# Reordered copies and shifts, and a gate and ranks of another shape, in a four-layer graph and expert kernel

## The chip, the cores and the metric

The kernel runs on one core of a Trainium2 chip. The metric is the device time of one execution in microseconds (us). The kernel before was timed in three runs. One further execution was recorded by the hardware profiler, and all views of the profile are of that one. The engines are named TensorE (PE; its weight loads are PEld), VectorE (DVE), ScalarE (ACT), GpSimd (POOL) and SyncE (SP, which here only issues loads and stores).

## The reference

Four layers work on x, 625 nodes with 512 values each, and each is added to x after a layer norm of its input:

```
x = x + gnn0(layernorm(x))    # hyperbolic graph convolution, twice
x = x + moe(layernorm(x))     # 8 experts, top 2 of a softmax gate, capacity 93
x = x + gnn1(layernorm(x))    # graph convolution, twice, relu between
x = x + attn(layernorm(x))    # 8 x 16 = 128 heads over 100 pooled keys, then a two-layer map
```

In gnn0 each row is mapped (`h = mobius_matvec(W, x)`), a bias is added in the hyperbolic sense (a scaled row plus a scaled bias row, here called the shift), and the rows of 10000 edges and of the nodes' own loops are summed with weights `dis[row] * dis[col]`, where dis is the degree to the power -0.5.

In moe, `probs = softmax(xf @ gate_w.T + gate_b)`; each node goes to its two best experts, and each expert takes the 93 nodes of the largest weight, those with a lower index first where weights are equal:

```
wm = where(routed, w_te, -1.0)
sel_w, sel_idx = top_k(wm.T, cap)
h = gelu(einsum('ecd,edh->ech', xf[sel_idx], w1) + b1)
out = einsum('ech,ehd->ecd', h, w2) + b2     # times sel_w, added back at sel_idx
```

In attn, for each head: `att = softmax(q k)`, `z = att vc`; over all heads z is normed by its l2 norm, scaled by wz_g1, and `h1 = silu(zn @ wz_w1 + wz_b1)` (16384 by 1024) follows, then a norm and `wz_w2`.

## The kernel before

[...] Instructions are recorded in the order of the code, some parts at a higher priority, and each engine runs its own queue in the order in which a scheduler has then put it. `order(later, sooner)` fixes the order of two instructions. `busy(ps, n, behind)` issues n matmuls whose result is not used.

**Adjacency counts (gnn0).** `one_hots(j)` takes the j-th column of 125 edges and lets VectorE build two fp16 tiles: `sh` (line 390), which marks the source of each edge, in a ring of 8, and `dh` (line 391), which marks the target. TensorE multiplies them with 5 matmuls a column into the `eps` banks (line 78 for all of the front's matmuls). There are 80 columns. The last 8 of the last group are built in `finished`: their one-hots first, then, at high priority, their products tile by tile, the row of degrees (`total`, `dps`, `dboth`, `ddigit`, `degs`), `dis`, and the tiles `digit` and `AT` of the adjacency matrix. Beside this `conv_in` prepares the rows: ScalarE scales `raw` (line 580) and VectorE adds the bias row times a factor (line 581, the shift), for 5 tiles. After `finished`, the rows are scaled by dis (line 486), and `agps` (line 592) multiplies AT by them.

**Experts' front (moe).** `xf` is the normed x, `xfT` its transpose (banks `trps`, line 296). For the gate, `gT` (512 by 8) is held as the weights and xfT is moved past it: `lps` (line 720), 8 by 375 and 8 by 250; ScalarE copies these to `lT` (line 721), and 5 transposes (line 723) bring them back to nodes by experts. VectorE adds the bias (`pr`, line 724), makes the softmax and marks the two best (`wm`, nodes by experts: weight or -1). Between these, on TensorE, stands work for the attention layer that needs nothing of it: transposes of the key weights (`wkps`, line 762, copied by ScalarE, line 763), `bops` (line 768) and `bbps` (line 780), which gives `hb`.

`ranked(e)` transposes expert e's column of wm to a row (`rowps`, line 795; `row`, line 797). Then for each tile of nodes two VectorE instructions over all 625 entries of the row count the nodes of a larger weight (`gt`, line 802), and those of an equal weight with a lower index (`eq`, line 805). For the latter, `before` (line 701, GpSimd, then line 703, VectorE) is a mask of 125 by 3125 in bf16. Their sum `rank` gives the slot of the node, and `take` (line 809) is the one-hot of slots. For expert 0, `gathered` multiplies xf by take (`xgps`, line 835) behind `busy` of 16 matmuls, and one copy takes the result to `xgT`. For the other experts the ranks run one expert ahead. `first_map` is line 865 (`hps`), `second_map` line 876 (`ops`).

**Attention.** 128 heads go in NB = 32 blocks of HB = 4. Iteration i of the loop records, in this order: loads for block i+1 (SP), `hidden(i-2)`, the transposes of heads 0 and 1 of block i-1, `folded(i)` (`kbps`, line 1151: keys through the query weights), `turned(i+1)`, then the four heads of block i-1, `prepared(i-1)`, and `scores(i)`:

```
for h in range(HB):
    valued = value(i - 1, h)
    if h + 2 < HB:
        transposes(i - 1, h + 2)
```

`transposes` (TensorE `atps`, line 1191) turns a head's attention, and ScalarE copies it to `attT` (line 1194, two copies of 375 and 250 columns). `value` multiplies (`zps`, line 1200, 4 records a head), ScalarE squares the result into `zs` (line 1203, one buffer), VectorE scales it into `zT` (line 1204), and GpSimd adds the square to `zsq` (line 1207; VectorE in the last block, line 1209). `prepared` makes sums and differences on VectorE: four of zT, and four over 1099 elements (lines 1214, 1215, 1217 and 1216, in that order), three of them into `zq`. `scores` are 40 matmul records `scps` (line 1164) in three groups; for each, VectorE adds `cb` into `att` (line 1165) and takes the maximum `a_top` (line 1167), and ScalarE the exponentials (line 1172). `hidden` is the large product with wz_w1 in a Strassen-like form: 98 small products `h1ps` (line 1263) of a block's zT and zq with wz or `wq`, its splits, which GpSimd makes (line 1223); VectorE adds the products to `hacc` (line 1275). At the start of a block's products TensorE reads zT twice and then zq of line 1216.

Of the kernel before, what the change touches and what calls it, by code (L numbers as in the profile page):

```python
# [28 lines left out]
DC = D // 128  # L29
# [139 lines left out]
def layers_kernel(  # L169
# [135 lines left out]
    def tp(t):  # L305
        return slice(t * P, (t + 1) * P)
# [7 lines left out]
    with ExitStack() as es:  # L314
# [58 lines left out]
        degs = big.tile([P, NT], F32, name="degs")  # L373
        V.memset(degs, 1.0)

        ahead = []

        def counting(first, last):

# [2 lines left out]
        def one_hots(j):  # L382

            sh = senders[j % HOT]
            dh = hot.tile([P, HALF], F16, tag="dh", name="dh")
            V.tensor_scalar(sh[:, :N], nodes, src_f[:, j : j + 1], None, op0=OP.is_equal)  # L390
            built = V.tensor_scalar(dh, nodes[:, :HALF], dst_f[:, j : j + 1], weight[:, j : j + 1],
                                    op0=OP.is_equal, op1=OP.mult)
            if j == AHEAD - 1:
                ahead.append(built)
            return j, sh, dh

        def counted(group, hots, i):
# [62 lines left out]
        def finished(group, columns):  # L460


            hots = [one_hots(j) for j in columns]
            both = work.tile([P, NT, HALF], I32, tag="both", name="both", bufs=1)
            with tc.high_priority():
                for i in (NT - 1, *range(NT - 1)):
                    for hot_pair in hots:
                        counted(group, hot_pair, i)
                    if i == NT - 1:
                        total = row_of(group)  # L470
                    A.activation(both[:, i, :], group[2][i][:P, :HALF], AF.Copy)
                    if i == 0:
                        degrees(total)

                        RP[0, NT].act(dis, degs, AF.Sqrt)
                        R.inverse(dis, dis)
                        for t in range(NT):
                            scaled(t, sent, dis)
            for i in range(NT):
                tiles_added(group[0], both, i, i + 1)  # L480
# [30 lines left out]
        def conv_in(k, turned, scale, inside, pieces, own=None, beside=None):  # L511
# [13 lines left out]
            for a, b in pieces:  # L525
# [52 lines left out]
                for t in range(a, b):  # L578
                    i = slice(t - a, t - a + 1)
                    A.activation(raw[:, t, :], raw[:, t, :], AF.Copy, scale=k1[:, i])  # L580
                    V.scalar_tensor_tensor(raw[:, t, :], b_row[k], x2[:, i], raw[:, t, :], op0=OP.mult, op1=OP.add)
            return raw, mapped

        def conv_out(raw, mapped, last):
# [89 lines left out]
    with ExitStack() as es:  # L674
# [19 lines left out]
        for piece in PIECES:  # L694
            for c in range(DC):
                transposed(psum, xfT[:, c, :], xf, c, pieces=(piece,), wait=None if c else (0, product))


        before = big.tile([P, NT, N], BF16, name="before")

        nc.gpsimd.iota(before, pattern=[[-P, NT], [1, N]], base=0, channel_multiplier=-1,
                       allow_small_or_imprecise_dtypes=True)
        V.tensor_scalar(before, before, 0.0, None, op0=OP.is_lt)
        slots = big.tile([P, CAP], F32, name="slots")
        nc.gpsimd.iota(slots, pattern=[[1, CAP]], base=0, channel_multiplier=0,
# [6 lines left out]


        pr = big.tile([P, NT, NE], F32, name="pr")
        lT = work.tile([NE, N], F32, name="lT", bufs=1)
        lps = psum.tile([128, 512], F32, tag="ps", name="ltps")
        for a, b in PIECES:
            ps = psum.tile([128, 512], F32, tag="ps", name="lps")
            for c in range(DC):
                T.matmul(ps[:NE, : (b - a) * P], gT[:, c, :], xfT[:, c, a * P : b * P], start=c == 0, stop=c == DC - 1)  # L720
            A.activation(lT[:, a * P : b * P], ps[:NE, : (b - a) * P], AF.Copy)
            for t in range(a, b):
                T.transpose(lps[:P, t * NE : (t + 1) * NE], lT[:, tp(t)], ident[:NE, :NE])
        V.tensor_tensor(pr, lps[:P, : NT * NE].rearrange("p (t e) -> p t e", e=NE),
                        gb[:, None, :].to_broadcast([P, NT, NE]), op=OP.add)
        top, tot = R.new("g_top"), R.new("g_tot")
# [48 lines left out]
            return product  # L775

        keys_map(range(1))
        ps = psum.tile([128, 512], F32, tag="ps", name="bbps")
        for g in range(G):
            T.matmul(ps[:L, :1], a1[:, g, :], bkT[:, g : g + 1], start=g == 0, stop=g == G - 1)  # L780
        V.tensor_tensor(hb, ps[:L, :1], a1b, op=OP.add)

        node = big.tile([P, NT], F32, name="node")
        nc.gpsimd.iota(node, pattern=[[P, NT]], base=0, channel_multiplier=1, allow_small_or_imprecise_dtypes=True)

# [2 lines left out]
        def ranked(e):  # L788


            row[e] = work.tile([P, N], F32, tag="row", name="row")
            for a, b in PIECES:
                ps = psum.tile([128, 512], F32, tag="ps", name="rowps")
                for t in range(a, b):
                    turned = T.transpose(ps[:P, (t - a) * P : (t - a + 1) * P],
                                         wm[:, t, e : e + 1].to_broadcast([P, P]), ident[:P, :P])
                A.activation(row[e][:, a * P : b * P], ps[:P, : (b - a) * P], AF.Copy)

            gt, eq = R.new("rk_gt"), R.new("rk_eq")
            for t in range(NT):  # L800
                junk = work.tile([P, N], F32, tag="junk", name="junk")
                V.tensor_scalar(junk, row[e], wm[:, t, e : e + 1], None, op0=OP.is_gt, op1=OP.add,
                                accum_out=gt[:, t : t + 1])
                junk = work.tile([P, N], F32, tag="junk", name="junk")
                V.scalar_tensor_tensor(junk, row[e], wm[:, t, e : e + 1], before[:, t, :], op0=OP.is_equal,
                                       op1=OP.mult, accum_out=eq[:, t : t + 1])
            R.add(rank[:, :, e], gt, eq)
            take[e] = work.tile([P, NT, CAP], F32, tag="take", name="take")
            V.tensor_tensor(take[e], slots[:, None, :].to_broadcast([P, NT, CAP]),
                            rank[:, :, e : e + 1].to_broadcast([P, NT, CAP]), op=OP.is_equal)  # L810
            return turned
# [13 lines left out]

        def gathered(e, behind=None):
            xgT[e] = work.tile([128, DC, CAP], F32, tag="xgT", name="xgT")
            ps = psum.tile([128, 512], F32, tag="ps", name="xgps")
            if e == 0:
                busy(ps, 16, behind)  # L830
            for c in range(DC):
                if e == 0:

                    for t in range(NT):
                        T.matmul(ps[:, c * CAP : (c + 1) * CAP], xf[:, t, c * 128 : (c + 1) * 128], take[e][:, t, :],
                                 start=t == 0, stop=t == NT - 1)
                    continue
                T.transpose(ps[:, c * CAP : (c + 1) * CAP], xg[e][:, c * 128 : (c + 1) * 128], ident[:CAP, :CAP])
            V.tensor_copy(xgT[e], ps[:, : DC * CAP].rearrange("p (c s) -> p c s", s=CAP))

# [67 lines left out]

        load(0)
        turned = ranked(0)  # L910
        gathered(0, keys_map(range(1, DC), turned))
        for e in range(NE):
            if e + 1 < NE:
                load(e + 1)
# [180 lines left out]
    with ExitStack() as es:  # L1095
# [89 lines left out]
        def transposes(b, h):  # L1185
            ps = banks("atps")
            if b == h == 0:
                busy(ps[:, 0], 13, folded.last)
            for k, (p0, p1) in enumerate(PIECES):
                for t in range(p0, p1):  # L1190
                    T.transpose(ps[:L, k, (t - p0) * P : (t - p0 + 1) * P], att[b][:, t, h * L : (h + 1) * L],  # L1191
                                ident[:P, :P])
            for k, (p0, p1) in enumerate(PIECES):
                A.activation(attT[h % 2][:, p0 * P : p1 * P], ps[:L, k, : (p1 - p0) * P], AF.Copy)  # L1194

        def value(b, h):
            g = b * HB // H
            ps = banks("zps")
            for u in range(2):
                T.matmul(ps[:, u, : 2 * QN], vc[:, g * DH : (g + 1) * DH], attT[h % 2][:, 2 * u * QN : 2 * (u + 1) * QN],  # L1200
                         start=True, stop=True)
            zs = work.tile([128, 2, 2 * QN], F32, tag="zs", name="zs", bufs=1)
            A.activation(zs, ps[:, :, : 2 * QN], AF.Square)  # L1203
            scaled = V.tensor_scalar(zT[:, h % 2 : 4 : 2, h // 2, :], ps[:, :, : 2 * QN], g1T[:, b * HB + h : b * HB + h + 1],  # L1204
                                     None, op0=OP.mult)
            if b < NB - 1:
                nc.gpsimd.tensor_tensor(zsq, zsq, zs.rearrange("p u s -> p (u s)"), op=OP.add)  # L1207
                return scaled
            return V.tensor_tensor(zsq, zsq, zs.rearrange("p u s -> p (u s)"), op=OP.add)
# [70 lines left out]
        for i in range(NB + 1):  # L1280
# [14 lines left out]
                turned(i + 1)  # L1295
            if i >= 1:
                for h in range(HB):
                    valued = value(i - 1, h)
                    if h + 2 < HB:
                        transposes(i - 1, h + 2)  # L1300
            if 1 <= i < NB:
                prepared(i - 1)
            if i < NB:
# [151 lines left out]
```

## Time and profile before

| | us |
|---|---|
| three runs | 2287.81, 2288.89, 2290.73 |
| median | 2288.89 |
| the profiled execution, its own time | 2287.9 |
| its span in the trace | 2286.1 |
| busy: PE, DVE, POOL, ACT | 2226.3, 1619.1, 992.1, 814.8 |

The span is the time from the first to the last recorded instruction; the execution's own time has 1.8 us more around it. A block of attention takes 50.32 us (the h1ps of one block starts at 1241.91 and of the next at 1292.23). The stretches that the change touches are, in the span of before, 66 to 110 us (one-hots and rows), 174 to 219 us (experts' front), 219 us to the end of the experts (later ranks), and 620 to 2187 us (the heads). In the rows, a name such as `zps<-attT,vc` is result and operands, xN the number of instructions, and `[.. <-..]` the idle time of the engine ahead of them with what ended it. In the groups of the page, `busy, mean ns | idle` follow the form. TensorE's granted clock is 1.00 of full speed in the experts' front and in the heads, 0.97 from 60 to 112 us.

### The profile page before, as it was taken

To read this page: it belongs to the slowest core of one execution; us is meant where nothing else is said; L and a number is where in the kernel's file an instruction comes from. 1 tells how busy PE (TensorE), PEld (TensorE's weight loads), DVE (VectorE), ACT (ScalarE), POOL (GpSimd) and SP (SyncE) were. 2 spreads that over 40 slices of the span, in tenths; PEclk is the share of its full clock that TensorE was granted. 3 is DMA by queue.
4 is the path that set the end of the run, shared out by engine and by line. 5 is a ranking of instruction groups with operands and counts; after the bars stand their busy time and mean duration, and the time that the engine had idled before them with its cause. 6 is when DMAs were issued, how large, how long until landed. Compare 5 with 4: busy or idle time off the path is not lost.

```text
span 2286.1 us, 34420 instructions
## 1 busy us (share of the span) xinstructions
PE 2226.3 (97%) x12812; PEld 1767.3 (77%) x12812; DVE 1619.1 (71%) x2303; ACT 814.8 (36%) x2773; POOL 992.1 (43%) x1063
## 2 busy tenths in 40 slices
PE   9999999999999999999999999999999999999987
PEld 6647666656788888888888888888888888888853
DVE  7846223233488888778888887788888778888782
ACT  3364111112334443343344334334433433344322
POOL 1000000200255666555566665555666565566531
PEclk9999999999999999999999999999999999999988
DMA  7002788670222222332222233222222332221110
GB/s 258 8 1 104 276 288 294 219 220 32 38 64 60 66 60 60 96 73 61 59 67 60 60 83 80 68 60 64 62 59 65 93 72 60 60 67 41 42 60 23
DMA packets 326026, 204.68 MB, mean 90 GB/s; under 512 B 275535, under 2 KB 279564, under 8 KB 321001
## 3 DMA queue, kind: packets, MB, share of 16 engines
q1 hardware_dynamic: 317371, 189.65, 28.3%
q10 hardware_dynamic: 3639, 7.56, 0.9%
q0 software_dynamic: 4848, 5.26, 0.8%
q8 instruction: 102, 1.67, 0.3%
q14 instruction: 66, 0.53, 0.1%
HBM read 197.18 MB, written 5.23 MB: 89 GB/s over the span
## 4 chain that ended last, share of the span: by engine, by line
PE 84%; DVE 6%; ACT 4%; POOL 2%; issue 2%; DMA 1%; POOLq 0%; ACTq 0%; SPq 0%; DVEq 0%
PE h1ps L1263 35%; PE scps L1164 18%; PE hps L865 5%; PE kbps L1151 5%; PE ops L876 5%; PE zps L1200 3%; POOL zsq L1207 2%; ACT zs L1203 2%; PE stps L959 2%; PE atps L1191 2%; PE l1ps L966 2%; PE agps L592 1%; DVE hacc L1311 1%; PE mxps L78 1%; PE eps L78 1%
## 5 line engine op out<-in xcount | busy, mean ns | idle before, releaser
L1275 DVE TENSOR_TENSOR hacc<-hacc,h1ps 128x942 f32<-128x942 f32 (+1 forms) x510 | 529.1, 1084 | 11.5 <-PE h1ps L1263 11.5
L1164 PE MATMUL scps<-keys,xnT 128*125 128x400 f32 x1280 | 435.1, 499 | 0.0
L1223 POOL TENSOR_TENSOR wq<-wz 128x256 f32<-128x256 f32 x248 | 241.3, 983 | 405.4 <-PE h1ps L1263 347.2
L1164 PEld LDWEIGHTS scps<-keys,xnT 128*125 128x125 f32 x1280 | 240.0, 188 | 185.0 <-issue 1.7
L1172 ACT ACTIVATE att<-att,a_top 125x100 f32<-125x100 f32 x640 | 231.9, 364 | 362.2 <-DVE a_top L1167 362.2
L1263 PE MATMUL h1ps<-zT,wq 128*128 128x157 f32 x1736 | 302.6, 296 | 0.0
L1263 PE MATMUL h1ps<-zq,wq 128*128 128x157 f32 x1736 | 302.5, 297 | 0.0
L1207 POOL TENSOR_TENSOR zsq<-zsq,zs 128x628 f32<-128x628 f32 x124 | 187.8, 1515 | 201.8 <-ACT zs L1203 201.8
L1263 PEld LDWEIGHTS h1ps<-zT,wq 128*128 128x128 f32 x1736 | 256.1, 189 | 0.0
L1263 PEld LDWEIGHTS h1ps<-zq,wq 128*128 128x128 f32 x1736 | 255.9, 190 | 0.0
L1194 ACT ACTIVATE attT<-atps 100x375 f32<-100x375 f32 (+1 forms) x256 | 92.7, 433 | 397.0 <-PE atps L1191 397.0
L1223 POOL TENSOR_TENSOR wq<-wz,wq 128x256 f32<-128x256 f32 x248 | 211.1, 851 | 19.4
L1204 DVE TENSOR_SCALAR zT<-zps,cols 128x628 f32<-128x628 f32 x128 | 111.6, 872 | 149.2 <-ACT zs L1203 147.8
L1183 ACT ACTIVATE att<-att,a_tot 125x100 f32<-125x100 f32 x620 | 170.2, 364 | 10.7 <-DVE a_tot L1173 10.7
L1200 PE MATMUL zps<-attT,vc 100*128 100x314 f32 x512 | 160.9, 436 | 10.7 <-ACT attT L1194 10.6
L1223 POOL TENSOR_TENSOR wq<-wsum,wq 128x256 f32<-128x256 f32 x186 | 161.6, 869 | 14.7 <-POOL wq L1223 0.3
L1223 POOL TENSOR_TENSOR wq<-wsum 128x256 f32<-128x256 f32 x186 | 136.1, 732 | 64.6 <-PE h1ps L1263 64.6
L1263 PE MATMUL h1ps<-zT,wz 128*128 128x157 f32 x992 | 152.5, 296 | 0.0
L1142 DVE STREAM_TRANSPOSE wqT<-wqraw 128x512 f32<-128x512 f32 x128 | 80.2, 681 | 101.0 <-PE kbps L1151 84.2
L1263 PEld LDWEIGHTS h1ps<-zT,wz 128*128 128x128 f32 x992 | 141.0, 189 | 9.1
L1203 ACT ACTIVATE zs<-zps 128x628 f32<-128x628 f32 x128 | 88.8, 694 | 125.0 <-POOL zsq L1207 111.2
L1200 PEld LDWEIGHTS zps<-attT,vc 100*128 100x128 f32 x512 | 87.4, 191 | 46.0 <-ACT attT L1194 27.0
(409 smaller groups left out, 3431.7 us busy)
## 6 DMA issues: line engine op xcount, KB each, us to landing
w<-in_L_ffn_w_dram SPq DMA_DIRECT2D x16, 4096.0 KB
wz<-in_L_ffn_wz_w_dram SPq DMA_DIRECT2D x32, 2048.0 KB
wqraw<-in_L_ffn_Wq_w_dram SPq DMA_DIRECT2D x512, 64.0 KB
cb<-qbias SPq DMA_DIRECT2D x32, 195.3 KB
wkv<-in_L_ffn_Wkv_w_dram SPq DMA_DIRECT2D x1, 4096.0 KB
W_raw<-in_L_gnn_W_dram SPq DMA_DIRECT2D x2, 1024.0 KB
w<-in_L_ffn_Wkv_w_dram SPq DMA_DIRECT2D x1, 2048.0 KB
l1w<-in_L_gnn_W_dram SPq DMA_DIRECT2D x2, 1024.0 KB
```

Source lines behind the costliest of these rows:

```text
L865: T.matmul(ps[:, i * CAP : (i + 1) * CAP], w1[e][:, c, hc * 128 : (hc + 1) * 128], xgT[e][:, c, :], start=c == 0, stop=c == DC - 1)
L876: T.matmul(ps[:CAP], hT[e][:, hc, :], w2[e][:, hc, :], start=hc == 0, stop=hc == HC - 1)
L1151: folded.last = T.matmul(ps[:, k, h * L : (h + 1) * L], wqT[b][h][:, (c + k) * 128 : (c + k + 1) * 128], kcT[:, b * HB // H, :], start=Tru ...
L1164: T.matmul(ps[:P, t - t0, : HB * L], xnT[:, c, tp(t)], keys[b][:, c, :], start=c == 0, stop=c == DC - 1)
L1172: A.activation(own, own, AF.Exp, bias=top[:, t, h : h + 1], accum_out=tot[:, t, h : h + 1])
L1183: A.activation(own, own, AF.Copy, scale=tot[:, t, h : h + 1])
L1200: T.matmul(ps[:, u, : 2 * QN], vc[:, g * DH : (g + 1) * DH], attT[h % 2][:, 2 * u * QN : 2 * (u + 1) * QN], start=True, stop=True)
L1203: A.activation(zs, ps[:, :, : 2 * QN], AF.Square)
L1207: nc.gpsimd.tensor_tensor(zsq, zsq, zs.rearrange("p u s -> p (u s)"), op=OP.add)
L1223: engine.tensor_tensor(to, x, y, op=OP.subtract)
L1263: T.matmul(ps[:, at % 6 // 3, at % 3 * QN : (at % 3 + 1) * QN], now[j][:, m * 128 : (m + 1) * 128], zquarter[b][j][:, place[i]], start=Tru ...
L1275: V.tensor_tensor(to, to, got, op=OP.add)
```

## The change

It has three parts.

1. In `value` for the second head, the transposes of the last head are recorded before the square, and the square is ordered behind the last head's copies.
2. The shifts of the rows (line 581 of before) are collected in a list, and each is ordered behind the last one-hot that was built.
3. In the experts' front: `before` is one mask of 125 by 125 in fp32. The gate holds the nodes (xfT) as weights and moves gT past them, 4 matmuls for each of 5 tiles, straight into nodes by experts; the copies to lT and the transposes are gone. A node's rank is counted in three parts: in the tiles in front of its own with "greater or equal", in its own tile and those behind with "greater", and in its own tile with "equal" times `before`. `bbps` is recorded behind `bops` and is what `busy` waits for, which has 3 matmuls for 16. The sum `hb` stands behind the last copy of xgT, and expert 0's xgT comes in four tiles with a copy each.

```diff
+            for op in shifted:
+                order(op, one_hots.last)
...
-        before = big.tile([P, NT, N], BF16, name="before")
+        before = big.tile([P, P], F32, name="before")
...
-        for a, b in PIECES:
-            ps = psum.tile([128, 512], F32, tag="ps", name="lps")
+        for t in range(NT):
             for c in range(DC):
-                T.matmul(ps[:NE, : (b - a) * P], gT[:, c, :], xfT[:, c, a * P : b * P], start=c == 0, stop=c == DC - 1)
-            A.activation(lT[:, a * P : b * P], ps[:NE, : (b - a) * P], AF.Copy)
-            for t in range(a, b):
-                T.transpose(lps[:P, t * NE : (t + 1) * NE], lT[:, tp(t)], ident[:NE, :NE])
+                T.matmul(lps[:P, t * NE : (t + 1) * NE], xfT[:, c, tp(t)], gT[:, c, :], start=c == 0, stop=c == DC - 1)
...
+            V.memset(ge[:, :1], 0.0)
             for t in range(NT):
+                own = wm[:, t, e : e + 1]
+                if t:
+                    junk = work.tile([P, N], F32, tag="junk", name="junk")
+                    V.tensor_scalar(junk[:, : t * P], row[e][:, : t * P], own, None, op0=OP.is_ge, op1=OP.add,
+                                    accum_out=ge[:, t : t + 1])
...
-                V.tensor_scalar(junk, row[e], wm[:, t, e : e + 1], None, op0=OP.is_gt, op1=OP.add,
+                V.tensor_scalar(junk[:, t * P :], row[e][:, t * P :], own, None, op0=OP.is_gt, op1=OP.add,
                                 accum_out=gt[:, t : t + 1])
...
-                V.scalar_tensor_tensor(junk, row[e], wm[:, t, e : e + 1], before[:, t, :], op0=OP.is_equal,
+                V.scalar_tensor_tensor(junk[:, tp(t)], row[e][:, tp(t)], own, before, op0=OP.is_equal,
                                        op1=OP.mult, accum_out=eq[:, t : t + 1])
+            R.add(gt, gt, ge)
             R.add(rank[:, :, e], gt, eq)
...
+            if e == 0:
+                for c in range(DC):
+                    ps = psum.tile([128, 512], F32, tag="ps", name="xgps")
+                    if c == 0:
+                        busy(ps, 3, behind)
+                    for t in range(NT):
+                        T.matmul(ps[:, :CAP], xf[:, t, c * 128 : (c + 1) * 128], take[e][:, t, :],
+                                 start=t == 0, stop=t == NT - 1)
+                    copied = V.tensor_copy(xgT[e][:, c, :], ps[:, :CAP])
+                return copied
...
+        turned = keys_map(range(1, DC), turned)
+        ps = psum.tile([128, 512], F32, tag="ps", name="bbps")
+        for g in range(G):
+            biased = T.matmul(ps[:L, :1], a1[:, g, :], bkT[:, g : g + 1], start=g == 0, stop=g == G - 1)
+            order(biased, turned)
+        last = gathered(0, biased)
+        order(V.tensor_tensor(hb, ps[:L, :1], a1b, op=OP.add), last)
...
+            turned_next = ahead() if ahead is not None else None
+            square = A.activation(zs, ps[:, :, : 2 * QN], AF.Square)
+            if turned_next is not None:
+                order(square, turned_next)
...
-                    valued = value(i - 1, h)
-                    if h + 2 < HB:
-                        transposes(i - 1, h + 2)
+                    valued = value(i - 1, h, (lambda: transposes(i - 1, 3)) if h == 1 else None)
+                    if h == 0:
+                        transposes(i - 1, 2)
```

More of the change, by code (lines that the diff above doesn't have):

```diff
@@ L374, in layers_kernel @@
         V.memset(degs, 1.0)
-        ahead = []
+        ahead, shifted = [], []
         def counting(first, last):
@@ L394, in one_hots @@
                 ahead.append(built)
+            one_hots.last = built
             return j, sh, dh
@@ L580, in conv_in @@
                     A.activation(raw[:, t, :], raw[:, t, :], AF.Copy, scale=k1[:, i])
-                    V.scalar_tensor_tensor(raw[:, t, :], b_row[k], x2[:, i], raw[:, t, :], op0=OP.mult, op1=OP.add)
+                    shifted.append(V.scalar_tensor_tensor(raw[:, t, :], b_row[k], x2[:, i], raw[:, t, :],
+                                                          op0=OP.mult, op1=OP.add))
             return raw, mapped
@@ L696, in layers_kernel @@
                 transposed(psum, xfT[:, c, :], xf, c, pieces=(piece,), wait=None if c else (0, product))
-        before = big.tile([P, NT, N], BF16, name="before")
-        nc.gpsimd.iota(before, pattern=[[-P, NT], [1, N]], base=0, channel_multiplier=-1,
-                       allow_small_or_imprecise_dtypes=True)
+        before = big.tile([P, P], F32, name="before")
+        nc.gpsimd.iota(before, pattern=[[1, P]], base=0, channel_multiplier=-1, allow_small_or_imprecise_dtypes=True)
         V.tensor_scalar(before, before, 0.0, None, op0=OP.is_lt)
@@ L714, in layers_kernel @@
         pr = big.tile([P, NT, NE], F32, name="pr")
-        lT = work.tile([NE, N], F32, name="lT", bufs=1)
         lps = psum.tile([128, 512], F32, tag="ps", name="ltps")
-        for a, b in PIECES:
-            ps = psum.tile([128, 512], F32, tag="ps", name="lps")
+        for t in range(NT):
             for c in range(DC):
-                T.matmul(ps[:NE, : (b - a) * P], gT[:, c, :], xfT[:, c, a * P : b * P], start=c == 0, stop=c == DC - 1)
-            A.activation(lT[:, a * P : b * P], ps[:NE, : (b - a) * P], AF.Copy)
-            for t in range(a, b):
-                T.transpose(lps[:P, t * NE : (t + 1) * NE], lT[:, tp(t)], ident[:NE, :NE])
+                T.matmul(lps[:P, t * NE : (t + 1) * NE], xfT[:, c, tp(t)], gT[:, c, :], start=c == 0, stop=c == DC - 1)
         V.tensor_tensor(pr, lps[:P, : NT * NE].rearrange("p (t e) -> p t e", e=NE),
@@ L777, in layers_kernel @@
         keys_map(range(1))
[L778 to L781, printed above, removed]
         node = big.tile([P, NT], F32, name="node")
@@ L797, in ranked @@
                 A.activation(row[e][:, a * P : b * P], ps[:P, : (b - a) * P], AF.Copy)
-            gt, eq = R.new("rk_gt"), R.new("rk_eq")
+            ge, gt, eq = R.new("rk_ge"), R.new("rk_gt"), R.new("rk_eq")
+            V.memset(ge[:, :1], 0.0)
             for t in range(NT):
+                own = wm[:, t, e : e + 1]
[3 more added lines that the diff above has]
+                                    accum_out=ge[:, t : t + 1])
                 junk = work.tile([P, N], F32, tag="junk", name="junk")
-                V.tensor_scalar(junk, row[e], wm[:, t, e : e + 1], None, op0=OP.is_gt, op1=OP.add,
+                V.tensor_scalar(junk[:, t * P :], row[e][:, t * P :], own, None, op0=OP.is_gt, op1=OP.add,
                                 accum_out=gt[:, t : t + 1])
                 junk = work.tile([P, N], F32, tag="junk", name="junk")
-                V.scalar_tensor_tensor(junk, row[e], wm[:, t, e : e + 1], before[:, t, :], op0=OP.is_equal,
+                V.scalar_tensor_tensor(junk[:, tp(t)], row[e][:, tp(t)], own, before, op0=OP.is_equal,
                                        op1=OP.mult, accum_out=eq[:, t : t + 1])
+            R.add(gt, gt, ge)
             R.add(rank[:, :, e], gt, eq)
@@ L827, in gathered @@
             xgT[e] = work.tile([128, DC, CAP], F32, tag="xgT", name="xgT")
+            if e == 0:
[8 more added lines that the diff above has]
+                return copied
             ps = psum.tile([128, 512], F32, tag="ps", name="xgps")
-            if e == 0:
-                busy(ps, 16, behind)
             for c in range(DC):
[L832 to L837, printed above, removed]
                 T.transpose(ps[:, c * CAP : (c + 1) * CAP], xg[e][:, c * 128 : (c + 1) * 128], ident[:CAP, :CAP])
@@ L910, in layers_kernel @@
         turned = ranked(0)
-        gathered(0, keys_map(range(1, DC), turned))
+        turned = keys_map(range(1, DC), turned)
[5 more added lines that the diff above has]
+        order(V.tensor_tensor(hb, ps[:L, :1], a1b, op=OP.add), last)
         for e in range(NE):
@@ L1193, in transposes, with value @@
             for k, (p0, p1) in enumerate(PIECES):
-                A.activation(attT[h % 2][:, p0 * P : p1 * P], ps[:L, k, : (p1 - p0) * P], AF.Copy)
-        def value(b, h):
+                copied = A.activation(attT[h % 2][:, p0 * P : p1 * P], ps[:L, k, : (p1 - p0) * P], AF.Copy)
+            return copied
+        def value(b, h, ahead=None):
             g = b * HB // H
@@ L1202, in value @@
             zs = work.tile([128, 2, 2 * QN], F32, tag="zs", name="zs", bufs=1)
-            A.activation(zs, ps[:, :, : 2 * QN], AF.Square)
+            turned_next = ahead() if ahead is not None else None
+            square = A.activation(zs, ps[:, :, : 2 * QN], AF.Square)
+            if turned_next is not None:
+                order(square, turned_next)
             scaled = V.tensor_scalar(zT[:, h % 2 : 4 : 2, h // 2, :], ps[:, :, : 2 * QN], g1T[:, b * HB + h : b * HB + h + 1],
```

## The prediction

> **What bounds the kernel now.** I read the busy shares first, then the chain that ended last, then three stretches of the chain beside the timeline: the attention loop, the experts' front and the build of the adjacency counts.
>
> ```profile
> PE 2226.3 (97%) x12812; PEld 1767.3 (77%) x12812; DVE 1619.1 (71%) x2303; ACT 814.8 (36%) x2773; POOL 992.1 (43%) x1063
> PE 84%; DVE 6%; ACT 4%; POOL 2%; issue 2%; DMA 1%; POOLq 0%; ACTq 0%; SPq 0%; DVEq 0%
> L1203 ACT ACTIVATE zs<-zps 128x628 f32<-128x628 f32 x128 | 88.8, 694 | 125.0 <-POOL zsq L1207 111.2
> L1200 PE MATMUL zps<-attT,vc 100*128 100x314 f32 x512 | 160.9, 436 | 10.7 <-ACT attT L1194 10.6
> ```
>
> TensorE works 97% of the span, so a change pays only where it closes a gap of TensorE's or shortens a chain that TensorE waits for. The last row is such a gap: zps waits for attT 10.6 us in all, 31 times, once a block. The row above it says why attT is late: ACT's square zs waits for GpSimd's sum of squares. One block in the chain of waits:
>
> ```profile
> 1224.48 1.53 POOL zsq L1207
> 1226.03 0.69 ACT zs L1203
> 1226.73 0.38 ACT attT L1194
> 1227.15 1.33 PE zps L1200 x4
> 1228.48 13.44 PE scps L1164 x40
> 1241.91 26.14 PE h1ps L1263 x196
> ```
>
> The second head's square starts at 1226.03, when zsq ends. The last head's copies, whose transposes ended at 1225.75, stand behind it on ACT's queue, and TensorE starts the last head's zps at 1227.15. The same block in the timeline, where h1ps begins:
>
> ```profile
> 1237.17 0.98 DVE L1165 TENSOR_TENSOR att<-scps,cb 125x800 f32<-125x800 f32 x1
> 1238.07 1.29 DVE L1215 TENSOR_TENSOR zq<-zq,zT 128x1099 f32<-128x1099 f32 x1
> 1239.28 1.30 DVE L1217 TENSOR_TENSOR zT<-zT 128x1099 f32<-128x1099 f32 x1
> 1240.49 1.29 DVE L1216 TENSOR_TENSOR zq<-zT,zq 128x1099 f32<-128x1099 f32 x1
> 1241.71 0.98 DVE L1167 TENSOR_REDUCE a_top<-att 125x8 f32<-125x800 f32 x1
> 1242.82 0.70 PE L1263 MATMUL h1ps<-zq,wz 128*128 128x157 f32 x4
> ```
>
> The zq of L1216 ends at 1241.79, and TensorE's third pair of products reads it at 1242.82: 1.03 us of slack. VectorE has run without an idle moment since 1231.39. A TensorE that comes earlier, or a VectorE that comes later, uses this slack up.
>
> **The attention loop, step by step.** The copies move ahead of the second head's square. They start when the transposes end: 1225.78 instead of 1226.62, two of 0.375 us, done at 1226.53. The first of the last head's zps, in a stream, follows the third head's at 4 x 0.267 = 1.07 us, at 1226.65, not 1227.15: 0.50 us, and the slow restart after the wait (1.33 us by the chain in place of about 1.23) gives 0.10 more. So TensorE reaches scps, and h1ps, 0.60 us earlier. Over 31 blocks this alone would be -18.6 us.
>
> Two things come later. First, the square waits behind the copies: 1226.41 instead of 1226.03 (between 0.35 and 0.50 later). zs has one buffer, and square, zsq, square, zsq run as one chain with GpSimd (the 1.53 and 0.69 above), so the last head's zs, and zT behind it, shift by the same 0.38. Second, the order of VectorE's instructions in the built program changes in all these blocks, which the diff doesn't say: a_top (L1167), in before behind that zq, now stands between the first zq and the second, and att ahead of the first. Ahead of the zq of L1216 there is thus one more instruction: spacing 0.90 us (att to zq, of 800 elements like a_top, is 1238.07 - 1237.17). It ends at 1241.79 + 0.38 + 0.90 = 1243.07, or 1242.94 with the spacings of each shape; I take 1242.94. TensorE arrives there at 1242.82 - 0.60 = 1242.22, and waits 0.72. With 0.05 for the release and 0.10 for the restart (as at zps) it goes on at 1243.10: **+0.28 us a block** against before. Range +0.15 (no restart cost) to +0.45 (0.13 later, square 0.04 later). The first such block had 0.55 of slack instead of 1.03: +0.75. Sum 30 x 0.28 + 0.75 = **+9.1 us**. Behind this point nothing else waits: att b, the next instruction of VectorE, shifts by about 0.35, and the third group of h1ps needs its bank 1.4 us after. GpSimd's splits and SP's loads keep their order and run ahead of need. In the last block the square of head 1 heads the chain into the final h1ps; the copy put in front of it costs 0.35 us: **+0.35**.
>
> **The experts' front.**
>
> ```profile
> 188.11 0.96 DVE L703 TENSOR_SCALAR before<-before 125x3125 bf16<-125x3125 bf16 x1
> 190.60 2.69 PE L720 MATMUL lps<-xfT,gT 128*8 128x375 f32 x8
> 197.06 0.20 DVE L724 TENSOR_TENSOR pr<-ltps,gb 125x40 f32<-125x40 f32 x1 [5.27 <-PE ltps L723]
> 201.83 1.49 PE L780 MATMUL bbps<-cols,a 128*100 128x1 f32 x16
> 203.19 0.79 PE L795 MATMUL rowps<-ident,wm 125*125 125x125 f32 x5
> 204.58 0.87 DVE L802 TENSOR_SCALAR_CACHE_REDUCE junk<-row,wm 125x625 f32<-125x625 f32 x1 [1.06 <-ACT row L797]
> 213.47 4.70 PE L835 MATMUL xgps<-take,xf 125*128 125x93 f32 x40 [0.57 <-DVE take L809]
> ```
>
> All of this lies on the chain. (1) The comparison at 188.11 shrinks from 3125 elements to 125 and moves ahead: the second half of the transposes comes 0.6 earlier (in the sum of the next step). GpSimd's iota that fills it shrinks too (2.81 us at 178.91), long before it is needed: nothing. (2) The gate: two groups of lps, two copies and five transposes become 20 matmuls with the nodes as weights (40 records, as 4 lps are 8). bbps is the nearest row: 16 records with 100 columns of weights and one moving column take 1.33 in the chain, 0.083 each; 0.104 for 125 columns, 4.2 us in all. [...] I follow the row. An ACT DMA issue (0.28) now stands ahead of the xfT copies, so the last xfT comes at about 191.5 (191.19). The gate ends at 195.1 and pr starts at 195.2: -1.85 (at 0.15 a record only -0.5). (3) The exponential stands behind one copy of w instead of two: -0.4. wm 202.3 becomes about 200.2. (4) bbps no longer stands ahead of rowps, which now waits for wm alone: 200.3, -2.9 in all. (5) Ranks: in before ten instructions at 0.787 spacing. 625/0.96 is 651 ns, so 0.136 is fixed. After: 14 instructions over 5 x 750 elements, 3.91 + 14 x 0.14 = 5.87, and one small sum 0.2. [...] -1.8. So xgps starts at 208.7: **-4.8**. TensorE's cover until then is bops 5.5, bbps 1.4 and the warm-up of 3 (0.7) behind rowps, ends at 208.7 too, so no gap opens that could lower the clock, but nothing more is to be gained there either. The hb sum behind them, the four small copies of xgT, the small memsets on VectorE and the b2 load issued earlier on ACT: 0 to -0.2. Weights' loads have slack behind bops, and the ranks of later experts lie beside hps (14.5 us an expert). Range -3.0 to -5.5.
>
> **The rows' shifts.**
>
> ```profile
> 77.27 3.40 DVE L581 SCALAR_TENSOR_TENSOR raw<-b_row,cv_x,raw 125x512 f32<-125x512 f32 x5
> 102.76 0.16 DVE L424 CAST dboth<-dps 125x3 int32<-125x3 f32 x1 [2.15 <-PE dps L78]
> ```
>
> They leave 77.27. VectorE builds a column in 0.58, TensorE uses it in 0.80, and the ring is eight deep, so VectorE was already waiting for slots there; only 1.15 of the 3.40 reach the last one-hot (99.49 becomes 98.34), and dboth. Behind it the five shifts fill the wait for the last counts, but two to three of them (0.66 each) stand between dboth, the degrees and the scaled rows, a chain that agps waits for at 109.39: +1.98 - 1.15 = +0.8; I take **+0.5**, range -1.2 to +1.2.
>
> **Sum.** 9.1 + 0.35 - 4.8 + 0.5 = +5.1. The profiled execution, 2287.9 (span 2286.1), becomes 2293.0; it lies 1.0 under the median 2288.9, so I predict **2294.0**.
>
> **Rivals.** A: the sum as above, chance 0.55; its own range is -1 to +9, 2288 to 2298. B, on the other side: VectorE's new order does not bind, because zq of L1216 is ready by 1242.22 (it decides at 0.72 us: if the chain from zs to zq is shorter by that). Then TensorE keeps its 0.60: -18.6 - 4.8 + 0.85, about 2266. For it: the row of 10.6 us and 31 waits; against: VectorE is gapless from 1231.39 on. Chance 0.15. C: the release costs nothing and the square is barely later, +0.15 a block: 4.6 + 0.35 - 4.8 + 0.5, 2290; or zq's end comes at the same time as TensorE, 2286. Chance 0.17. D: the wait is dearer (0.45 a block) or GpSimd and VectorE slow each other: +14 - 4 = +10, 2299. Chance 0.13.
>
> **Numbers.** 0.2% is 4.6 us, about what a measurement of this kernel can tell from no change. Slower by more: somewhat over half of A (0.35) and D (0.13), 0.48. Within: the rest of A (0.18) and most of C (0.13), 0.31. Faster: B, and the low part of C and A, 0.21. The range 2283 to 2302 leaves out B and the far ends.
>
> **To look for after.** Right: zps no longer waits for attT; h1ps waits for zq on VectorE about 0.7 a block; period 50.6 instead of 50.32; xgps at about 208.7 less what the shifts did. Wrong: no idle before h1ps' third pair and a period of 49.7; or shorter gaps of agps at 109.

## The result and the profile after

The changed kernel takes 2295.22 us (median of 8 runs, 2294.2 to 2297.73) against 2288.77 of before (8 runs): a ratio of 1.0032, 95% interval 1.0022 to 1.0041. That is 6.4 us slower. The prediction was 2294.0, slower. The profiled execution has a span of 2293.1 us.

The rows of the page that answer to those of before:

```profile
PE 2224.8 (97%) x12805; PEld 1773.0 (77%) x12805; DVE 1605.4 (70%) x2386; ACT 818.0 (36%) x2771; POOL 989.8 (43%) x1063
PE 67%; DVE 19%; ACT 6%; POOL 4%; issue 3%; DMA 1%; ACTq 0%; POOLq 0%; DVEq 0%; SPq 0%
L1216 ACT ACTIVATE zs<-zps 128x628 f32<-128x628 f32 x128 | 89.0, 695 | 114.7 <-POOL zsq L1222 100.7
L1212 PE MATMUL zps<-attT,vc 100*128 100x314 f32 x512 | 152.5, 430 | 0.1
```

The gap at zps is closed (10.7 us of idle time became 0.1), and still VectorE's share of the chain went from 6% to 19%. The chain of waits in a block shows how it runs now:

```profile
1224.66 0.76 ACT attT L1204 x2
1225.41 0.59 ACT zs L1216
1226.07 1.52 POOL zsq L1222
...
1237.30 0.90 DVE a_top L1177
...
1240.62 1.22 DVE zq L1231
1241.88 25.34 PE h1ps L1278 x188
```

The copies stand ahead of the square, a_top stands between the parts of zq, and h1ps goes on only when zq (line 1231, line 1216 of before) ends. The view of waits, with the sum, the number and the longest in us, has the price of that, 0.70 us in each of 31 blocks:

```profile
PE h1ps L1278 <- DVE zq L1231: 21.7, 31, 0.7
```

A block takes 50.67 us (50.32 before). In the experts' front, the timeline rows that answer to those of before:

```profile
194.52 0.20 DVE L722 TENSOR_TENSOR pr<-ltps,gb 125x40 f32<-125x40 f32 x1 [5.59 <-PE ltps L721]
201.10 0.73 PE L788 MATMUL rowps<-ident,wm 125*125 125x125 f32 x5
202.43 0.86 DVE L802 TENSOR_SCALAR_CACHE_REDUCE junk<-row,wm 125x625 f32<-125x625 f32 x1 [2.88 <-ACT row L790]
209.34 4.70 PE L836 MATMUL xgps<-take,xf 125*128 125x93 f32 x40
```

rowps has no idle time of TensorE's ahead of it: wm was ready at 199.56, and TensorE came at 201.10. The table by windows (us, busy time and instructions of PE, PEld, DVE, ACT, POOL, then the granted clock, the DMA share, GB/s) says why:

```profile
188.00:190.00 2.00, 1.89 (x18) 1.91 (x18) 0.94 (x3) 1.73 (x5) 0.00 (x0) 1.00 0.32 105
190.00:192.00 2.00, 2.00 (x18) 2.00 (x18) 0.00 (x0) 0.02 (x1) 0.00 (x0) 0.86 0.36 135
192.00:194.00 2.00, 2.00 (x11) 2.00 (x11) 0.00 (x0) 0.00 (x0) 0.00 (x0) 0.50 0.33 128
...
196.00:198.00 2.00, 2.00 (x11) 2.00 (x10) 1.90 (x5) 1.27 (x3) 0.00 (x0) 0.50 0.33 128
198.00:200.00 2.00, 2.00 (x19) 2.00 (x18) 1.42 (x7) 1.94 (x4) 0.00 (x0) 0.94 0.06 24
```

TensorE is busy in all but 0.11 us of these windows, but its clock falls to half while the gate's matmuls run, and 11 instructions fall into a window of 2 us instead of 18.

The two profiled executions also differ where the change touched nothing: before had TensorE at a clock of 0.57 from 33 to 36 us and 0.66 from 555 to 560 us, where the changed one had 1.00. That gave the changed execution 2.1 us by the end of the first group of counts (its `dboth`), and 1.8 more between the experts and the heads. It is a matter of the single execution, not of the change: e1, e2 and e3, whose code is before's in this stretch, reached the same mark 1.6 to 2.3 us earlier too. The experiments are therefore read stage by stage, each stage from a mark of its own.

### The profile page after: what moved, and what is told of

It reads as the page before. It is cut to its first block, busy times and chain, and to the rows that moved or that the text cites. A ratio compares the mean times of both kernels' runs of the same rounds, so it can differ in the third digit from the quotient of the medians.

```text
span 2293.1 us, 34516 instructions
## 1 busy us (share of the span) xinstructions
PE 2224.8 (97%) x12805; PEld 1773.0 (77%) x12805; DVE 1605.4 (70%) x2386; ACT 818.0 (36%) x2771; POOL 989.8 (43%) x1063
## 3 DMA queue, kind: packets, MB, share of 16 engines
q0 software_dynamic: 4848, 5.26, 0.8%
## 4 chain that ended last, share of the span: by engine, by line
PE 67%; DVE 19%; ACT 6%; POOL 4%; issue 3%; DMA 1%; ACTq 0%; POOLq 0%; DVEq 0%; SPq 0%
PE h1ps L1278 34%; PE hps L869 5%; PE kbps L1161 5%; PE ops L880 5%; POOL zsq L1222 4%; PE zps L1212 3%; PE atps L1201 3%; ACT zs L1216 3%; PE stps L969 2%; DVE zT L1229 2%; DVE zT L1232 2%; DVE zq L1231 2%; DVE zq L1229 2%; DVE zq L1230 2%; PE eps L78 2%
## 5 line engine op out<-in xcount | busy, mean ns | idle before, releaser
L1290 DVE TENSOR_TENSOR hacc<-hacc,h1ps 128x942 f32<-128x942 f32 (+1 forms) x510 | 534.5, 1085 | 36.0 <-PE h1ps L1278 31.8
L1193 ACT ACTIVATE att<-att,a_tot 125x100 f32<-125x100 f32 x620 | 170.1, 364 | 10.7 <-DVE a_tot L1183 10.7
L1212 PE MATMUL zps<-attT,vc 100*128 100x314 f32 x512 | 152.5, 430 | 0.1
L1161 PE MATMUL kbps<-kcT,wqT 128*128 128x100 f32 x1024 | 122.0, 277 | 0.3 <-DVE hacc L1290 0.3
```

The costliest lines, as they stand in the source:

```text
L1161: folded.last = T.matmul(ps[:, k, h * L : (h + 1) * L], wqT[b][h][:, (c + k) * 128 : (c + k + 1) * 128], kcT[:, b * HB // H, :], start=Tru ...
L1193: A.activation(own, own, AF.Copy, scale=tot[:, t, h : h + 1])
L1290: V.tensor_tensor(to, to, got, op=OP.add)
```

## The experiments

All were timed in five rounds beside before. Two stage times from the profile go with them: a block of the heads (zps to zps), and the front, from the end of the last agps to the first hps (40.03 us before, 37.57 in the changed kernel).

**e1, the copies alone**: the first part of the change, on the kernel before.

> The kernel before with the first part alone (last head's copies ahead of the second head's square). Theory (VectorE's new order binds: a_top ahead of the zq that TensorE reads third): TensorE waits about 0.70 us for that zq in each of 31 blocks, a block takes 50.67 us instead of 50.32, and the last block 0.35 more: +11.2, about 2300. Rival (the loop is neutral and the 6.4 us of the changed kernel come from elsewhere): 2289.

Measured: 2299.07, ratio 1.0049 (1.0035 to 1.0063), +10.7 us; 50.67 a block. The loss is that of the first part, and at the size of the theory. The cause was not yet shown by it.

**e2, the copies with zq first.**

```diff
+            zsums.third = V.tensor_tensor(to[2], z[0][1], to[1], op=OP.subtract)
...
+                peak = V.tensor_reduce(top[:, t0:t1, :].rearrange("p t h -> p (t h)"),
+                if b and t0 == 0:
+                    order(peak, zsums.third)
```

> As the copies alone, but the first a_top of each block is ordered behind that zq, as VectorE's queue had it before. Theory (order): zq is ready at about 1242.17 in the block of the prediction, TensorE comes at 1242.22: next to no wait, a block takes 49.7 to 49.8 us, -17 us, about 2272. Rival (the later square and the chain of squares behind it are what TensorE waits for, not the order): the wait stays at 0.4 or more and the time is 2284 or above.

Measured: 2300.6, ratio 1.0055 (1.0041 to 1.0068). My theory fell, by 28 us. The first block took 49.97 us, as the theory has it, but from the second on it was 50.71. The wait for zq was gone (0.20 was still lost there), and TensorE waited in another place, at the end of the block. Timeline rows of one block of e2, then the rows of before that answer to the first two, with its one wait for h1ps:

```profile
1229.14 0.87 DVE L1211 TENSOR_SCALAR zT<-zps,cols 128x628 f32<-128x628 f32 x1 [1.90 <-ACT zs L1208]
1252.47 0.28 DVE L1175 RECIPROCAL a_tot<-a_tot 125x20 f32<-125x20 f32 x1 [1.27 <-ACT att L1174]
1269.40 0.70 PE L1193 MATMUL atps<-ident,att 125*100 125x125 f32 x5
1270.30 0.74 PE L1193 MATMUL atps<-ident,att 125*100 125x125 f32 x5 [0.20 <-DVE hacc L1282]
1271.35 3.81 PE L1151 MATMUL kbps<-kcT,wqT 128*128 128x100 f32 x32 [0.30 <-DVE hacc L1282]
```

```profile
1226.76 0.87 DVE L1204 TENSOR_SCALAR zT<-zps,cols 128x628 f32<-128x628 f32 x1 [1.45 <-ACT zs L1203]
1250.10 0.28 DVE L1173 RECIPROCAL a_tot<-a_tot 125x20 f32<-125x20 f32 x1 [1.27 <-ACT att L1172]
1254.75 1.14 DVE L1275 TENSOR_TENSOR hacc<-hacc,h1ps 128x942 f32<-128x942 f32 x1 [0.26 <-PE h1ps L1263]
```

VectorE's second zT comes 0.45 later in the block than before (its idle time is 1.90, not 1.45), since the square does. From there to its last hacc its waits are for ScalarE and as long as in before (1.45 twice for zs, 1.27 for a_tot), so it is late at the end, and the transposes and kbps that reuse its banks wait. In before VectorE had only 0.26 us to spare in a block, the one time it waited for h1ps. In numbers: TensorE gains 0.60 at zps, loses 0.20 at zq, where it arrives at the very moment zq does, and 0.80 between atps and kbps (1.95 from start to start instead of 1.14): +0.40; the block grew by 0.39.

**e3, the order alone**: the second zq ordered behind the first a_top (`order(zsums.second, peak)`), nothing else.

> The kernel before with VectorE's order alone: a_top is ordered ahead of the second zq, the copies stay where they were. Theory (slack): zq comes 0.8 to 0.9 us later into 1.03 us of slack, TensorE does not wait, 50.32 us a block, 2289 (within 2). Rival (an instruction more ahead of zq costs its 0.9 us wherever it stands): +27, 2316.

Measured: 2294.55, ratio 1.0026 (1.0017 to 1.0035); a block 50.46, the first one 1.38 longer. Both expectations missed. zq ends 1.0 us later, and TensorE meets it: 0.03 of wait, and the second matmul behind it comes after 0.24 instead of 0.13 (the four take 0.80, in before 0.70):

```profile
1244.64 0.80 PE L1265 MATMUL h1ps<-zq,wz 128*128 128x157 f32 x4
```

These 0.14 in 30 blocks and the first block make the 5.6 us that the loop is longer. A slack that is used up to the last hundredth is not free.

**e4, the changed kernel with zq first**: the edit of e2 on the changed kernel.

> The changed kernel with the first a_top of each block ordered behind the zq. Theory (order): the changed kernel's 2295.2 less 31 times 0.9 us: about 2267, clear below before. Rival (the later square): 2284 or above.

Measured: 2293.34, ratio 1.0027 (1.0017 to 1.0037); 50.71 a block, as e2. So it is not VectorE's order that keeps the first part from paying; the order only decides where TensorE waits.

**e9, as e4, with a_tot later.**

```diff
+            shares[b] = V.reciprocal(tot, tot)
...
+                                if at == 6 * 5 and b + 1 in shares:
+                                    order(shares[b + 1], added_up)
```

> e4 (the changed kernel, zq ahead of the first a_top) with one thing more: a_tot, for which VectorE waits 1.27 us in e2 and e4 because ScalarE's exponentials aren't done, is ordered behind the fifth hacc of the block instead of the third. Theory (the block is a closed loop through VectorE, which is 0.45 late from the second square on and hands its banks back late): VectorE regains 1.27, TensorE is the bound again, 49.7 us a block, about 2263. Rival (VectorE's lateness isn't what holds e4): 50.7 us a block as in e4, 2293.

Measured: 2271.24, ratio 0.9924 (0.9911 to 0.9938); 49.90 a block. VectorE doesn't wait for a_tot any more, gives its banks back in time, and the 0.80 between atps and kbps are gone:

```profile
1242.37 0.27 DVE L1186 RECIPROCAL a_tot<-a_tot 125x20 f32<-125x20 f32 x1
1259.70 3.81 PE L1162 MATMUL kbps<-kcT,wqT 128*128 128x100 f32 x32
```

The block is -0.60 + 0.20 = -0.40 against before; the missing 0.20 to 49.7 is the meeting at zq, as in e2. The theory of the closed loop holds: VectorE's work of a block, once late at the squares, hands TensorE its banks back late.

**e8, two buffers for zs.**

```diff
-            zs = work.tile([128, 2, 2 * QN], F32, tag="zs", name="zs", bufs=1)
+            zs = work.tile([128, 2, 2 * QN], F32, tag="zs", name="zs", bufs=2)
```

> The kernel before with two buffers for zs instead of one; every engine's queue keeps its order (but for the last block). Theory (the block is a closed loop through VectorE, of which the chain of squares sets the start): squares no longer wait for GpSimd's sums, the second square runs at about 1225.1 of the block of the prediction instead of 1226.0 and the last scaled zT comes 1 to 3 us earlier, so neither attT nor VectorE holds TensorE: 49.7 us a block, -18 us, 2270. Rival (VectorE is bound by its own work, whatever comes first): 50.1 us or more a block, 2281 or above.

Measured: 2267.21, ratio 0.9912 (0.9898 to 0.9925), with no instruction moved in the blocks. The chain of a block:

```profile
1216.37 2.12 PE zps L1200 x8
1218.49 13.44 PE scps L1164 x40
1231.93 26.14 PE h1ps L1263 x196
1258.07 1.07 PE atps L1191 x10
1259.14 3.73 PE kbps L1151 x32
```

It is TensorE from end to end, 49.70 us. Squares follow zps at once, the copies follow in time, the last zT starts 2.7 us earlier in the block (6.33 instead of 9.03 after the first zps), and VectorE now waits for TensorE, not TensorE for it:

```profile
DVE hacc L1275 <- PE h1ps L1263: 59.3, 128, 0.5
```

**e10, the changed kernel with two buffers for zs.**

> The changed kernel with two buffers for zs (rk_ge takes the place of a tile no longer used, for room). Theory (one buffer, and the chain of squares that it makes, was what the moved copies delayed): 49.7 us a block with the copies ahead of the square too, e5 less 21, 2263. Rival (the copies ahead of the square cost by themselves, or VectorE's order does): 50.3 or more a block, 2284 or above.

Measured: 2262.71, ratio 0.9889 (0.9874 to 0.9904); 49.70 a block. With a second buffer the copies ahead of the square cost nothing, and gain nothing.

**e5, the second and third part without the first**: the changed kernel with the heads of before.

> The second and third part without the first: the changed kernel's front, the heads as before. Prediction's sum for these parts: 0.5 - 4.8 = -4.3, 2284.1. By the two profiles (the changed one has TensorE's clock at 0.50 from 191.4 to 198.6 us, and is only 2.4 us ahead behind the experts' front): +0.1 - 2.5 = -2.4, 2286.

Measured: 2284.07, ratio 0.998 (0.9971 to 0.9989), -4.6 us. In the profile the front is 2.47 us shorter (37.56). The rest of the 4.6 isn't in the stages that these parts touch; the interval reaches from -6.6 to -2.5.

**e6, the gate with more columns.**

```diff
+                T.matmul(lps[:P, t * 64 : (t + 1) * 64].rearrange("p (k e) -> p k e", e=NE), xfT[:, c, tp(t)],
+                         gT[:, c, None, :].to_broadcast([128, 64 // NE, NE]), start=c == 0, stop=c == DC - 1)
```

> As e5, but each matmul of the gate moves gT eight times over, 64 columns instead of 8, into 64 columns of the bank (the first 8 are used): the same number of matmuls and weight loads, with more of the array at work. Theory (the clock falls because TensorE's matmuls move 8 columns, so that it counts as idle): the clock stays at 1.0, a gate record takes 0.104 us, and expert 0 begins about 2.4 us earlier than in e5: 2283.6. Rival (the clock falls for another reason, such as the phase of the run or the weight loads): the clock falls to 0.5 here too and the time is e5's or, with wider matmuls, above it.

Measured: 2280.93, ratio 0.9966 (0.9954 to 0.9978). The front takes 34.87 us, 2.69 less than in e5. The windows over its gate and the wkps behind it:

```profile
191.00:193.00 2.00, 2.00 (x17) 1.90 (x18) 0.75 (x3) 0.96 (x3) 0.00 (x0) 1.00 0.32 108
193.00:195.00 2.00, 2.00 (x20) 2.00 (x20) 0.00 (x0) 0.00 (x0) 0.00 (x0) 1.00 0.36 135
195.00:197.00 2.00, 2.00 (x21) 2.00 (x21) 0.65 (x4) 0.80 (x3) 0.00 (x0) 1.00 0.33 128
197.00:199.00 2.00, 2.00 (x21) 2.00 (x20) 1.86 (x6) 2.00 (x5) 0.00 (x0) 1.00 0.33 128
```

The same number of matmuls with eight times the columns runs at full clock. That TensorE counts as idle under 8 columns was the theory's guess, and no run shows it. What the runs show is the clock: with the 8-column gate it is 0.50 in the windows from 192 to 198 us in the changed kernel, from 192 to 196 in e4 and e5 and from 194 to 200 in e9; with 64 columns it is 1.00 in all windows from 191 to 199 in e6 and from 188 to 200 in e11. With the old gate it is 1.00 from 186 to 214 in before and from 180 to 208 in e7; in e12 it is 0.50 from about 187.4 to 190.9, ahead of most of its gate, behind windows in which TensorE had worked only 1.64 of 3.40 us. So a half clock can fall into this stretch with the old gate too, but with the 8 columns it came in each of these four profiles, and with TensorE at work (2.00 of 2.00 us in every window at 0.50).

**e7, the old gate with the rest of parts 2 and 3.**

> As e5, but with the gate as before (gT as the weights, copies to lT, transposes). Theory (clock): no half speed in this stretch; the gate's own gain (-0.6 in the profile) is given up, and rowps, no longer held by TensorE at half speed, comes 1.5 to 2.5 earlier than in e5 for its queue and 0.6 later for wm: about e5 less 1, 2285. Rival (the new gate is worth its 1.85 us of the prediction): e5 plus 1.8, 2288.

Measured: 2283.27, ratio 0.9978 (0.9969 to 0.9987); front 36.64, 0.92 less than in e5, as the theory of the clock had it. The times of e5 and e7 do not tell the two apart. The gate's own worth shows against e6: 36.64 - 34.87 = 1.77 us.

**e12, the shifts alone**: the second part of the change, on the kernel before.

> The kernel before with the second part alone (shifts behind the one-hots). Prediction: +0.5 (-1.2 to +1.2). By the profiles of the changed kernel (0.15 later at agps than its lead at the first group of counts): +0.1, 2288.8. Rival (the shifts' 3.40 us come off in full): 2285.3.

Measured: 2287.26, ratio 0.9995 (0.9986 to 1.0004). From the first group of counts to the last one-hot it takes 43.65 us instead of 44.82, and to the ninth matmul record of agps 55.50 instead of 55.67. The 3.40 us do not come off; what does is mostly given back. How much isn't sure to some tenths: in the profiles of before, e1, e2 and e8, whose code is the same here, the second of these times runs from 55.65 to 56.31.

**e11, the parts that pay**: e6 with two buffers for zs, the heads otherwise as before.

> e6 (parts 2 and 3, wide gate) and e8 (two zs buffers) in one, heads otherwise as before. The two lie in different stretches, so their gains add: 2280.9 - 21.5 = 2259.5. Rival (TensorE, now without gaps in the heads, draws something else down): above 2263.

Measured: 2259.99, ratio 0.9874 (0.9859 to 0.9889): 28.5 us faster than before. The gains of e6 (7.8) and e8 (21.5) add up to 29.2, so they hardly touch each other. Its page:

```profile
PE 2213.9 (98%) x12805; PEld 1770.2 (78%) x12805; DVE 1633.4 (72%) x2386; ACT 813.7 (36%) x2771; POOL 991.9 (44%) x1063
PE 90%; DVE 5%; ACT 2%; issue 2%; DMA 1%; POOLq 0%; SPq 0%; DVEq 0%; ACTq 0%; POOL 0%
```

## Why the prediction was right, and where it was not

| term of the sum | predicted | measured |
|---|---|---|
| heads, 31 blocks | +9.1 | +11.6 (changed kernel), +10.7 (e1) |
| last block and behind | +0.35 | +0.33 to its third pair of h1ps, +1.8 to the last (changed kernel) |
| experts' front | -4.8 | -2.46, and -5.16 with the clock at 1.0 (e6) |
| shifts | +0.5 | +0.1 (changed kernel), -0.2 (e12) |
| sum | +5.1 | +6.4 |

**The heads: cause right, one term too small.** TensorE comes to scps 0.60 earlier (5.34 after the first zps instead of 5.95), as predicted. zq ends 20.65 after the first zps, against 20.58 in the prediction, and TensorE waits 0.70 against 0.72. The matmuls around the wait take 0.97 more in all, so the block is +0.36 and not +0.28: the mis-sized term is the release and restart, 0.15 in the sum, 0.27 measured (0.97 - 0.70). One block of the changed kernel was 0.74 longer than its neighbours: in it a wsum on VectorE took 1.71 instead of 1.27 us while a wq on GpSimd took 1.72 instead of 0.73, and TensorE waited for the late hacc before atps and kbps. Rival D named such a case, GpSimd and VectorE slowing each other; that they did is not shown, and why it was this block alone stays open. Of the +1.8 behind the heads, 1.4 goes with the clock of this one execution: 48 records of h1ps took 14.64 us instead of 13.23, with the clock at 0.53 for the first 3.6 of them.

The sentence that behind this point nothing else waits holds for the changed kernel (one wait of 0.3 us for kbps in all its blocks, in the long one), but only with VectorE's new order. What failed is the reasoning behind rival B: I compared VectorE with TensorE at zq alone, and took it that without the new order TensorE would keep its 0.60. e2 and e4 refuted that. VectorE is a second bound of the block with 0.26 us to spare, and the square's delay of 0.45 alone makes it late at the banks of atps and kbps. The new order moved that cost: it has a_top earlier, so ScalarE's exponentials and then a_tot come earlier (VectorE waits 0.30 for a_tot in e1, 1.27 in e2 and in before), and VectorE gets back at a_tot what TensorE pays at zq. With either order a block loses 0.35 to 0.39. Two edits show it from both ends, and either is enough: e9, with zq first, takes VectorE's wait for a_tot away (49.90), e8 the single buffer that ties the squares to GpSimd (49.70).

**The front: the gain halved by the clock.** The steps hold where the clock does: in e6 pr is 1.95 earlier in its stage (predicted 1.85), rowps 2.88 (2.9), hps 5.16 (4.8). The ranks' instruction of 625 elements comes at 0.787 in before, and in the changed kernel those of 500, 375, 250 and 125 at 0.65, 0.52, 0.39 and 0.26, which is 1.04 ns an element (0.96 elements a ns) and 0.13 to 0.14 fixed; before has the same 1.04 in its att, 0.981 for 800 elements and 0.565 for 400. The whole fell from 7.9 to 5.9. What failed is that a gate record was priced at full clock throughout. While the clock was full it cost 0.109 (0.104 predicted), at half 0.21; in the changed kernel 34 of them took 5.26 us, 0.155 on average, and pr was only 0.59 earlier: the upper bound that I had named and set aside. The half clock then reached wkps behind it (28 in 5.16 us instead of 3.28), so rowps was held by TensorE and only 0.14 earlier. I had asked for idle gaps around bops, and not what a busy TensorE with 8 columns does to the clock. Gaps do stand ahead of each half clock in before: it is 0.50 from 33.4, 98.3, 555.6, 2187.2, 2221.4 and 2272.6 us, and in the 3.40 us ahead TensorE was busy for 1.08, 1.28, 2.14, 1.49, 0.86 and 1.05. In the changed kernel the clock fell about 3.3 us after the gate's first matmul (188.11 to about 191.4, worked out from the 0.86 of its window), with TensorE busy for 3.32 of the 3.40 us ahead.

**The shifts**: the last one-hot came 1.17 earlier (1.15 predicted). dboth and agps gave back 1.0 of it or more; +0.5 was too much by 0.4 to 0.7.

**The sum, and luck in it.** By the medians the first part is +10.7 (9.1 + 0.35 predicted) and the other two together -4.6 (-4.3 predicted), 6.1 in all. By the stages of the two profiled executions the parts come to 11.6 + 1.8 - 2.5 + 0.1 = 11.0, of which the stretches where only before's clock had fallen take 3.9 off again, which leaves the 7.0 between the spans. So by the stages the loss in the heads and the gain in the front were missed by some 2 us each, both towards slower, and the chance in this pair of executions was 3.9 us the other way and 1.4 (above) this way. The medians are near the sum because the other two parts gain about 2 us there that no stage shows: -4.6 in e5 against -2.5 by its stages; e6 and e7 too are 7.8 and 5.4 faster, with fronts only 5.2 and 3.4 shorter. Where these 2 us lie isn't settled; that the sum came so near is in part luck.

## What to carry to other kernels

When a move takes away one wait in a loop, follow the other engines once around: an engine that hands buffers back at the end is a second bound, and its slack is the time for which it waits in a block for the engine that it serves (VectorE for TensorE's products: 0.26 us here), not its waits for a third engine and not the slack at one tile. If a copy and a square compete for a place in a queue, ask first what makes the square late: here it was a single buffer, and a second one was worth 21 us where the reordering lost 11. Before matmuls are made narrow, look at the granted clock under them (here 0.50 with 8 moving columns in the changed kernel, 1.00 with 64 in e6), and not only at whether TensorE is busy.

## What the runs showed of the hardware

- In the changed kernel the clock fell to 0.50 under matmuls of 125 weight columns and 8 moving columns, with TensorE busy for 3.89 of 4.00 us, and stayed there for about 6.8 us (to about 198.2, from the 0.94 of its window). It was 0.50 there in e4, e5 and e9 too, which have the same 8 columns; with 64 moving columns, in e6 and e11, it stayed at 1.00.
- In e3 a TensorE that had to wait only 0.03 us for an operand lost 0.14: the second matmul after the wait came after 0.24 us instead of 0.13. After the 0.70 us of the changed kernel it was 0.24 too.
